# One outer product of a fast-weight recurrence, moved from GpSimd to VectorE

## The chip, the cores and the metric

The kernel runs on one core of a Trainium2 chip. Its time is the device time of one execution in microseconds (us). A core has five engines, each with an instruction queue of its own that it works off strictly in order: TensorE (PE, its weight loads PEld) for matrix products into PSUM, VectorE (DVE), ScalarE (ACT), GpSimd (POOL), and SyncE (SP), which issues the DMA transfers here. Engines wait for one another through semaphores. In the profile, L534 is line 534 of the kernel.

## The reference

Two blocks are applied to x of shape 16 x 512 x 256 (batch, time, channels). The second block (attention in a window of 64 and a gated mixing of channels) and the low-rank feed-forward network of the first are not touched. The part that matters is the attention of the first block, a recurrence over chunks of 16 tokens with 16 heads of 16 channels. Each head carries two small matrices of 4 inner rows, `W_in` and `W_out`:

```python
def step(carry, xs):
    W_in, W_out = carry
    q_t, k_t, v_t, lr_t = xs
    ...
    W_out = W_out + jnp.einsum('bnhD,bnhd->bDhd', k_h, v_t)
    lr_in = lr_t[:, :1, :, 0:1]
    lr_out = lr_t[:, :1, :, 1:2]
    for _ in range(2):
        g_out = -attn(W_in, k_t, v_t)
        g_in = -attn(W_out, v_t, k_t)
        W_in = W_in - lr_in * g_in
        W_out = W_out - lr_out * g_out
    return ((W_in, W_out), o_t)
```

`attn(W_out, v_t, k_t)` scores the 4 rows of `W_out` against the 16 tokens `v_t`, takes the softmax over the tokens, and sums the tokens `k_t` with these weights. It is used twice in a step, with two successive `W_out`; both sums are added to `W_in`. Nothing of a step can start before the `W_in` and `W_out` that it needs are there.

## The kernel before

A unit of work is one half of the batch (8 sequences) and 64 time steps; there are 16 units, which alternate between the halves. A unit goes through five streams: `prepare` (norm, projections, convolution), `chain` (the recurrence, 4 chunks of 16 tokens, `recur`), `mlp`, `attend` and `mix`. `timetable` gives each stream its times, so that in the text of the program the chains of two units, one of each half, run side by side, while earlier and later units go through the other streams. The scheduler of the language then orders each engine's instructions by its own estimate of when they can run, so the order on an engine is not that of the text.

In the recurrence the 128 partitions are the 8 sequences by 16 heads of one half. A product of 4 rows, 16 channels and 16 tokens is 1024 elements for each partition. A sum over tokens is made in two instructions: `outer` (L530 to L535) multiplies weights and tokens, both spread by broadcasting, into a buffer, on GpSimd; `total` (L634 to L637) sums that buffer over its last axis on VectorE. Scores (L523 to L528) are a product and a reduction, both on VectorE. The matrices `w_in` and `w_out` (tile `fw`) lie in PSUM; the tokens, the weights and the product buffers lie in SBUF. The product buffers are a ring of five for both halves (`big`, L520).

A step does this in order:

- L602 to L613: scores of k and q with `w_in`, the first softmax (weights `e_k`), the softmax over inner rows (`hid`).
- L615 and L626: two outer products on GpSimd, `pd_o` and `pd_kv`.
- L628 to L632: `pd_kv` is summed up along the tokens with a scan on VectorE.
- L641 to L644: `w_out` after the first inner step; scores of v with both versions of `w_out`, and exponentials `e_v` for both (2 x 4 rows).
- L646: `over_tokens` turns `e_v` into weights; its last instruction is L549.
- L647: the two outer products `pd_i`, one for each inner step, with the tokens `dt_k`, both on GpSimd. In the text the first stands before the second.
- L649: the sum `di` of the first product (L636) is added to `w_in`.
- L651 and L652: scores of k with this `w_in`, and the exponentials of the second softmax.
- L653: the sum of the second product is added to `w_in`. This is the `w_in` of the next step.
- L655 and L657: the last outer product `pd_o` on GpSimd; its sum is added to `w_out` early in the next step.
- L661 to L663: the outputs of the chunk, three products and sums on GpSimd.

GpSimd also adds residuals (`x` L389), squares (`ka` L1055), copies the rows that the convolution carries over (`xp` L453, `tails` L456), splits maxima (L215 and L217) and takes the root for the norms (`rs` L350 and L351). VectorE also does the convolution (L460), the maxima of the attention's scores (L889), the mixing (`mix` L1033), and norms (L347, L348, L353).

Of the kernel before, what the change touches and what calls it, by code (L numbers as in the profile page):

```python
# [17 lines left out]
P = 128  # L18
B, T, C = 16, 512, 256
H, D, R = 16, 16, 4  # L20
CH = 16
# [74 lines left out]
def adaln_blocks(ctx: ExitStack, tc: tile.TileContext, a: dict, out: bass.AP):  # L96
    nc = tc.nc
    mul, add, sub = ALU.mult, ALU.add, ALU.subtract
# [295 lines left out]
    def place(u):  # L394

        return u % NH, u // NH
# [120 lines left out]
    def small(half, name, n):  # L517
        return rec.tile([P, n], F32, tag=f"s{n}_{half}", name=name, bufs={XW: 5, 2 * XW: 3}.get(n, 4))

    def big(half, name):  # L520
        return rec.tile([P, R * D * CH], F32, tag="prod", name=name, bufs=5)

    def scores(half, engine, tok, w, dst, tag):  # L523

        pr = big(half, f"sc_{tag}").rearrange("p (r t d) -> p r t d", r=R, t=CH)
        every = [P, R, CH, D]
        engine.tensor_tensor(pr, tok.unsqueeze(1).to_broadcast(every), w.unsqueeze(2).to_broadcast(every), mul)  # L527
        nc.vector.tensor_reduce(dst, pr, AX.X, add)  # L528

    def outer(half, engine, hid, tok, tag):  # L530

        pr = big(half, f"pd_{tag}").rearrange("p (r d t) -> p r d t", r=R, d=D)
        every = [P, R, D, CH]
        engine.tensor_tensor(pr, hid.unsqueeze(2).to_broadcast(every), tok.unsqueeze(1).to_broadcast(every), mul)  # L534
        return pr  # L535

    def exp_tokens(half, s, n, mx, tag):

        nc.vector.tensor_reduce(mx, s, AX.X, ALU.max)
        e = small(half, f"e_{tag}", n * CH).rearrange("p (r t) -> p r t", t=CH)  # L540
        nc.vector.tensor_tensor(e, s, mx.unsqueeze(2).to_broadcast([P, n, CH]), sub)
        nc.scalar.activation(e, e, AF.Exp, scale=1.0 / math.sqrt(D))
        return e

    def over_tokens(half, e, n, rate, sm):

        nc.vector.tensor_reduce(sm, e, AX.X, add)
        nc.vector.reciprocal(sm, sm)
        nc.vector.scalar_tensor_tensor(e, e, rate, sm.unsqueeze(2).to_broadcast([P, n, CH]), mul, mul)  # L549
        return e  # L550
# [36 lines left out]
    def recur(u, pc, c, s):  # L587

        half = place(u)[0]
        f = fws[half]  # L590
        tag = f"{u}_{pc}_{c}"
        cs = slice(c * CH, (c + 1) * CH)
        k_dt, v_dt, q_dt, lr = s["k"][:, :, cs], s["v"][:, :, cs], s["q"][:, :, cs], s["lr"]
        lr_in, lr_out = lr[:, 0, c * CH : c * CH + 1], lr[:, 1, c * CH : c * CH + 1]
        tok = rec.tile([P, 3, CH, D], F32, tag=f"tok_{half}", name=f"tok{tag}", bufs=1)
        for n, x in enumerate((k_dt, q_dt, v_dt)):
            nc.scalar.copy(tok[:, n], x.rearrange("p d t -> p t d"))  # L597
        k, q, v = (tok[:, n] for n in range(3))
        w_in, w_out, w_outs = f["w_in"], f["w_out"], f["w_outs"]

        sc = small(half, f"scs{tag}", 2 * XW).rearrange("p (r t) -> p r t", r=R)
        scores(half, nc.vector, k, w_in, sc[:, :, :CH], f"k{tag}")  # L602
        scores(half, nc.vector, q, w_in, sc[:, :, CH:], f"q{tag}")
        late[half]()
        p_out = exp_tokens(half, sc[:, :, :CH], R, f["mx_k"], f"k{tag}")


        mx = f["hid"]
        nc.vector.tensor_reduce(mx, sc.rearrange("p r t -> p t r"), AX.X, ALU.max)
        hid = small(half, f"hid{tag}", R * 2 * CH).rearrange("p (r t) -> p r t", r=R)  # L610
        every = [P, R, 2 * CH]
        nc.vector.tensor_tensor(hid, sc, mx.unsqueeze(1).to_broadcast(every), sub)
        nc.scalar.activation(hid, hid, AF.Exp)  # L613
        yield
        d_out = outer(half, nc.gpsimd, over_tokens(half, p_out, R, lr_out, f["sm_k"]), v_dt, f"o1{tag}")  # L615

        sm = f["hid"][:, :CH]
        kh, qh = hid[:, :, :CH], hid[:, :, CH:]
        nc.vector.tensor_reduce(sm, kh.rearrange("p r t -> p t r"), AX.X, add)
        nc.vector.tensor_reduce(s["sum"][:, cs], qh.rearrange("p r t -> p t r"), AX.X, add)  # L620
        nc.vector.reciprocal(sm, sm)
        nc.vector.tensor_tensor(sm, sm, lr[:, 1, cs], mul)
        nc.vector.tensor_tensor(kh, kh, sm.unsqueeze(1).to_broadcast([P, R, CH]), mul)  # L623


        kv = outer(half, nc.gpsimd, kh, v_dt, f"kv{tag}")  # L626
        yield
        nc.vector.tensor_tensor(kv[:, :, :, 0], kv[:, :, :, 0], w_out, add)  # L628
        upto = kv
        flat = kv.rearrange("p r d t -> p (r d t)")  # L630
        nc.vector.tensor_tensor_scan(flat, within, flat, 0.0, mul, add)  # L631
        nc.vector.tensor_copy(w_outs[:, :R], upto[:, :, :, CH - 1])  # L632

        def total(pr, name):  # L634
            t = small(half, f"{name}{tag}", XW).rearrange("p (r d) -> p r d", r=R)
            nc.vector.tensor_reduce(t, pr, AX.X, add)  # L636
            return t  # L637


        sv = small(half, f"sv{tag}", 2 * XW).rearrange("p (r t) -> p r t", t=CH)  # L640
        nc.vector.tensor_tensor(w_outs[:, R:], total(d_out, "do1"), w_outs[:, :R], add)  # L641
        for n in range(2):
            scores(half, nc.vector, v, w_outs[:, n * R : (n + 1) * R], sv[:, n * R : (n + 1) * R], f"v{n}{tag}")
        p_in = exp_tokens(half, sv, 2 * R, f["mx_v"], f"v{tag}")  # L644
        yield
        p_in = over_tokens(half, p_in, 2 * R, lr_in, f["sm_v"])  # L646
        d_in = [outer(half, nc.gpsimd, p_in[:, n * R : (n + 1) * R], k_dt, f"i{n}{tag}") for n in range(2)]  # L647
        yield
        nc.vector.tensor_tensor(w_in, total(d_in[0], "di0"), w_in, add)  # L649
        sk = small(half, f"sk{tag}", XW).rearrange("p (r t) -> p r t", t=CH)  # L650
        scores(half, nc.vector, k, w_in, sk, f"k2{tag}")  # L651
        p_out = exp_tokens(half, sk, R, f["mx_k"], f"k2{tag}")  # L652
        nc.vector.tensor_tensor(w_in, total(d_in[1], "di1"), w_in, add)  # L653
        yield
        d_out = outer(half, nc.gpsimd, over_tokens(half, p_out, R, lr_out, f["sm_k"]), v_dt, f"o2{tag}")  # L655
        yield
        late[half] = lambda: nc.vector.tensor_tensor(w_out, total(d_out, "do2"), w_outs[:, R:], add)  # L657


        po = upto  # L660
        nc.gpsimd.tensor_tensor(po, qh.unsqueeze(2).to_broadcast([P, R, D, CH]), upto, mul)  # L661
        nc.gpsimd.tensor_tensor(po[:, :2], po[:, :2], po[:, 2:], add)
        nc.gpsimd.tensor_tensor(q_dt, po[:, 0], po[:, 1], add)  # L663
# [435 lines left out]
    def chain(u):  # L1099

        for m in range(NPC):
            piece = load_piece(u, m)
            for c in range(CPP):
                yield from recur(u, m, c, piece)
                if c == CPP - 1:
                    finish_piece(u, m, piece)
                yield
# [87 lines left out]
```

## Time and profile before

| | us |
|---|---|
| time, median of 3 runs | 3226.88 |
| lowest and highest of them | 3222.9 and 3235.52 |
| the profiled execution's own time | 3231.29 |
| its span, first to last instruction | 3229.5 |
| mean granted TensorE clock in it | 0.822 |

Three more groups of the recurrence, as the page has them:

```profile
L534 POOL TENSOR_TENSOR pd_o<-e_k,dt_v 128x1024 f32<-128x1024 f32 x128 | 301.0, 2358 | 171.4 <-DVE e_k L549 171.3
...
L661 POOL TENSOR_TENSOR pd_kv<-hid,pd_kv 128x1024 f32<-128x1024 f32 x64 | 150.3, 2349 | 165.6 <-DVE fw L632 141.6
...
L631 DVE TENSOR_TENSOR_SCAN pd_kv<-within,pd_kv 128x1024 f32<-128x1024 bf16 x64 | 174.4, 2725 | 0.9
```

A line gives the source line, the engine, the operation, output and inputs by name, their shapes, the count; then the busy time of the group in us and the mean of one in ns; then the idle time of the engine just before these instructions, and what ended it. The first line says that 128 outer products took 301.0 us on GpSimd, and that GpSimd had stood idle 171.4 us in front of them, nearly all of it for the weights `e_k` from VectorE. In a timeline a line gives start and duration in us first, and in brackets the idle time before it with its releaser. In a line by source or tile, the three numbers after the count are the least, the median and the greatest duration in ns.

### The profile page before, as it was taken

The page shows a single profiled execution, that of the slowest core. Times are in us where ns is not written, and L with a number is a line of the kernel's source. Part 1 is how long each engine was busy: PE and PEld are TensorE (multiplying, and loading weights), DVE is VectorE, ACT ScalarE, POOL GpSimd, SP SyncE. Part 2 cuts the span into 40 slices and gives each one's busy share as a digit, 9 for nine tenths or more (in the row PEclk, how much of TensorE's full clock was granted, in tenths as well). Part 3 has the DMA queues.
Part 4 walks back from the last instruction along what each step waited for, and adds up shares of the span by engine and source line. Part 5 has one row for each costly group of instructions (what it writes and reads, how often), then busy time and mean ns, then how long its engine had stood idle before and what let it go on. Part 6 is the DMA issues. An engine that isn't in the chain of part 4 may idle for free.

```text
span 3229.5 us, 47324 instructions
## 1 busy us (share of the span) xinstructions
PE 2385.4 (74%) x17232; PEld 1452.9 (45%) x17232; DVE 2395.3 (74%) x4513; ACT 1783.6 (55%) x3748; POOL 1673.0 (52%) x1575
## 2 busy tenths in 40 slices
PE   3540156868787776887788887889787888788996
PEld 2210123444444454554445554555445555555664
DVE  1688787878787787778888888888888878774221
ACT  1761354556665745565564666566664655445543
POOL 0245556556556655555556564555555655654112
PEclk7775676878797887888888798979888887879998
DMA  5420112132314132131313223230402212122010
GB/s 151 94 58 13 47 37 67 31 73 55 80 36 94 32 83 54 51 83 33 88 27 72 69 59 75 51 83 27 100 21 72 62 51 56 45 52 60 17 28 27
DMA packets 439307, 186.46 MB, mean 58 GB/s; under 512 B 323937, under 2 KB 413090, under 8 KB 439074
## 3 DMA queue, kind: packets, MB, share of 16 engines
q1 hardware_dynamic: 439074, 183.44, 23.2%
q8 instruction: 135, 2.21, 0.3%
q14 instruction: 98, 0.80, 0.1%
HBM read 116.66 MB, written 66.72 MB: 57 GB/s over the span
## 4 chain that ended last, share of the span: by engine, by line
DVE 33%; PE 22%; POOL 20%; ACT 12%; issue 8%; DMA 4%; SPq 1%; POOLq 0%; DVEq 0%; ACTq 0%
POOL pd_o L534 5%; POOL pd_i L534 4%; DVE pd_kv L631 4%; DVE sc_v L527 3%; POOL pd_kv L534 3%; DVE sv L528 3%; DVE do L636 2%; PE st L873 2%; DVE di L636 2%; DVE sc_k L527 2%; DVE pp L460 2%; PE pproj L1005 2%; DMA oT<-o 2%; DVE scs L528 2%; DVE mx L889 1%
## 5 line engine op out<-in xcount | busy, mean ns | idle before, releaser
L534 POOL TENSOR_TENSOR pd_o<-e_k,dt_v 128x1024 f32<-128x1024 f32 x128 | 301.0, 2358 | 171.4 <-DVE e_k L549 171.3
L534 POOL TENSOR_TENSOR pd_i<-e_v,dt_k 128x1024 f32<-128x1024 f32 x128 | 298.4, 2369 | 43.4 <-DVE e_v L549 43.4
L708 PE MATMUL pwo<-w_WoT,oT 128*128 128x256 f32 x256 | 106.6, 576 | 223.0 <-POOL oT L701 201.8
L873 PE MATMUL st<-qs,keys 32*128 32x128 f32 x2048 | 191.3, 336 | 71.7 <-DVE yT L983 29.0
L661 POOL TENSOR_TENSOR pd_kv<-hid,pd_kv 128x1024 f32<-128x1024 f32 x64 | 150.3, 2349 | 165.6 <-DVE fw L632 141.6
L873 PE MATMUL sc<-keys,qs 32*128 32x128 f32 x2048 | 183.1, 326 | 71.7 <-DVE mx L889 41.7
L636 DVE TENSOR_REDUCE do<-pd_o 128x64 f32<-128x1024 f32 x126 | 152.3, 1213 | 102.5 <-POOL pd_o L534 102.5
L636 DVE TENSOR_REDUCE di<-pd_i 128x64 f32<-128x1024 f32 x128 | 155.1, 1214 | 88.3 <-POOL pd_i L534 88.3
L873 PEld LDWEIGHTS st<-qs,keys 32*128 32x128 f32 x2048 | 160.5, 226 | 132.2 <-DVE mx L889 32.4
L873 PEld LDWEIGHTS sc<-keys,qs 32*128 32x128 f32 x2048 | 148.0, 216 | 141.9 <-DVE mx L889 58.8
L889 DVE TENSOR_REDUCE mx<-sc 128x4 f32<-128x512 f32 x256 | 168.2, 679 | 26.2 <-PE sc L870 26.2
L708 PEld LDWEIGHTS pwo<-w_WoT,oT 128*128 128x128 f32 x256 | 68.4, 287 | 250.7 <-POOL oT L701 218.3
L534 POOL TENSOR_TENSOR pd_kv<-hid,dt_v 128x1024 f32<-128x1024 f32 x64 | 151.4, 2366 | 54.7 <-DVE hid L623 50.0
L926 ACT ACTIVATE pT<-st 128x512 f32<-128x512 f32 x256 | 135.3, 605 | 73.7 <-PE st L870 73.4
L631 DVE TENSOR_TENSOR_SCAN pd_kv<-within,pd_kv 128x1024 f32<-128x1024 bf16 x64 | 174.4, 2725 | 0.9
L527 DVE TENSOR_TENSOR sc_k<-tok,fw 128x1024 f32<-128x1024 f32 x128 | 155.4, 1214 | 14.8 <-ACT tok L597 13.5
L527 DVE TENSOR_TENSOR sc_v<-tok,fw 128x1024 f32<-128x1024 f32 x128 | 150.3, 1215 | 1.6
L224 ACT ACT_TABLE_LOAD x111 | 142.4, 1283 | 14.3 <-PE ph L736 7.6
L528 DVE TENSOR_REDUCE sv<-sc_v 128x64 f32<-128x1024 f32 x128 | 149.6, 1209 | 0.0
L736 PE MATMUL ph<-PT,w_v 64*128 64x512 f32 x256 | 111.1, 669 | 38.0 <-ACT z L224 27.8
L1005 PE MATMUL pproj<-w_proj,yT 128*128 128x256 f32 x512 | 122.9, 386 | 11.2 <-DVE yT L983 9.3
L197 PE MATMUL pmx<-w_w_attnT,blocks 128*128 128x384 f32 x256 | 118.5, 593 | 13.4 <-ACT hp L367 9.4
(251 smaller groups left out, 6827.7 us busy)
## 6 DMA issues: line engine op xcount, KB each, us to landing
values<-values SPq DMA_DIRECT2D x56, 256.0 KB
gate_a<-gates SPq DMA_DIRECT2D x64, 128.0 KB
xa<-in_x_dram SPq DMA_DIRECT2D x32, 256.0 KB
x<-in_x_dram SPq DMA_DIRECT2D x32, 256.0 KB
gate_c<-gates SPq DMA_DIRECT2D x64, 128.0 KB
gate_d<-gates SPq DMA_DIRECT2D x64, 128.0 KB
q<-y SPq DMA_DIRECT2D x64, 128.0 KB
dt_q<-q SPq DMA_DIRECT2D x32, 256.0 KB
```

The costliest lines, as they stand in the source:

```text
L224: ins = nc.scalar.activation(*args[0], **args[1])
L527: engine.tensor_tensor(pr, tok.unsqueeze(1).to_broadcast(every), w.unsqueeze(2).to_broadcast(every), mul)
L528: nc.vector.tensor_reduce(dst, pr, AX.X, add)
L534: engine.tensor_tensor(pr, hid.unsqueeze(2).to_broadcast(every), tok.unsqueeze(1).to_broadcast(every), mul)
L631: nc.vector.tensor_tensor_scan(flat, within, flat, 0.0, mul, add)
L636: nc.vector.tensor_reduce(t, pr, AX.X, add)
L661: nc.gpsimd.tensor_tensor(po, qh.unsqueeze(2).to_broadcast([P, R, D, CH]), upto, mul)
L708: nc.tensor.matmul(po[:, n * C : (n + 1) * C], lhsT=pair(oT, k, 2 * b2 + n), rhs=w_o[:, k, :], start=k == 0, stop=k == 1,)
L873: nc.tensor.matmul(dst, lhsT=lhsT, rhs=rhs, start=start, stop=False, skip_group_check=True)
L889: nc.vector.tensor_reduce(mx[:, j], sc[j].rearrange("p (s k) -> p s k", s=NS), AX.X, ALU.max)
L926: nc.scalar.activation(pT[j], st[j], AF.Exp)
L1005: nc.tensor.matmul(po[:, n * C : (n + 1) * C], lhsT=yT[:, k2, par].rearrange("p e t -> p (e t)"), rhs=w_proj[:, k2, par, :], start=k2 == 0 ...
```

## The change

`outer` takes a list of engines instead of one, and shares the 4 inner rows out among them in equal parts. The first `pd_i` gets the list with VectorE alone, the second the list with GpSimd alone; all other outer products get GpSimd alone. With a list of one, `n` is 4 and the product is one instruction of 1024 elements as before. In the changed kernel the multiplication of `outer` is at L537, the last instruction of `over_tokens` at L554, `total` at L641, and the additions to `w_in` at L657 and L661.

```diff
-    def outer(half, engine, hid, tok, tag):
+    def outer(half, engines, hid, tok, tag):
 
         pr = big(half, f"pd_{tag}").rearrange("p (r d t) -> p r d t", r=R, d=D)
-        every = [P, R, D, CH]
-        engine.tensor_tensor(pr, hid.unsqueeze(2).to_broadcast(every), tok.unsqueeze(1).to_broadcast(every), mul)
+        n = R // len(engines)
+        every = [P, n, D, CH]
+        for k, engine in enumerate(engines):
+            part = slice(k * n, (k + 1) * n)
+            engine.tensor_tensor(
+                pr[:, part], hid[:, part].unsqueeze(2).to_broadcast(every), tok.unsqueeze(1).to_broadcast(every), mul
+            )
         return pr
...
-        d_in = [outer(half, nc.gpsimd, p_in[:, n * R : (n + 1) * R], k_dt, f"i{n}{tag}") for n in range(2)]
+        d_in = [
+            outer(half, engines, p_in[:, n * R : (n + 1) * R], k_dt, f"i{n}{tag}")
+            for n, engines in enumerate(([nc.vector], [nc.gpsimd]))
+        ]
```

The other three calls (`o1`, `kv`, `o2`) change `nc.gpsimd` to `[nc.gpsimd]` and nothing else.

More of the change, by code (lines that the diff above doesn't have):

```diff
@@ L614, in recur @@
         yield
-        d_out = outer(half, nc.gpsimd, over_tokens(half, p_out, R, lr_out, f["sm_k"]), v_dt, f"o1{tag}")
+        d_out = outer(half, [nc.gpsimd], over_tokens(half, p_out, R, lr_out, f["sm_k"]), v_dt, f"o1{tag}")
         sm = f["hid"][:, :CH]
@@ L623, in recur @@
         nc.vector.tensor_tensor(kh, kh, sm.unsqueeze(1).to_broadcast([P, R, CH]), mul)
-        kv = outer(half, nc.gpsimd, kh, v_dt, f"kv{tag}")
+        kv = outer(half, [nc.gpsimd], kh, v_dt, f"kv{tag}")
         yield
@@ L654, in recur @@
         yield
-        d_out = outer(half, nc.gpsimd, over_tokens(half, p_out, R, lr_out, f["sm_k"]), v_dt, f"o2{tag}")
+        d_out = outer(half, [nc.gpsimd], over_tokens(half, p_out, R, lr_out, f["sm_k"]), v_dt, f"o2{tag}")
         yield
```

## The prediction

> **What bounds the kernel now.** I read the page first: busy shares, the slices, the chain that ended last, the costliest groups.
>
> ```profile
> PE 2385.4 (74%) x17232; PEld 1452.9 (45%) x17232; DVE 2395.3 (74%) x4513; ACT 1783.6 (55%) x3748; POOL 1673.0 (52%) x1575
> ...
> DVE  1688787878787787778888888888888878774221
> ...
> DVE 33%; PE 22%; POOL 20%; ACT 12%; issue 8%; DMA 4%; SPq 1%; POOLq 0%; DVEq 0%; ACTq 0%
> POOL pd_o L534 5%; POOL pd_i L534 4%; DVE pd_kv L631 4%; DVE sc_v L527 3%; POOL pd_kv L534 3%; DVE sv L528 3%; DVE do L636 2%; PE st L873 2%; DVE di L636 2%; DVE sc_k L527 2%; DVE pp L460 2%; PE pproj L1005 2%; DMA oT<-o 2%; DVE scs L528 2%; DVE mx L889 1%
> ...
> L534 POOL TENSOR_TENSOR pd_i<-e_v,dt_k 128x1024 f32<-128x1024 f32 x128 | 298.4, 2369 | 43.4 <-DVE e_v L549 43.4
> ...
> L636 DVE TENSOR_REDUCE di<-pd_i 128x64 f32<-128x1024 f32 x128 | 155.1, 1214 | 88.3 <-POOL pd_i L534 88.3
> ...
> L527 DVE TENSOR_TENSOR sc_k<-tok,fw 128x1024 f32<-128x1024 f32 x128 | 155.4, 1214 | 14.8 <-ACT tok L597 13.5
> ```
>
> VectorE is 70 to 80% busy from slice 3 until the recurrence ends, and it stands first in the chain. GpSimd is half idle, but what VectorE waits for is often a GpSimd product: 88.3 us of idle time stand before the reductions `di`. So the span is VectorE's queue, its work plus its waits. Then I read the timeline where the change acts. The two halves of the batch run in step: 30 pairs of steps, and 4 single ones at the ends. This is a pair with no other work between:
>
> ```profile
> 1105.58 0.35 DVE L549 SCALAR_TENSOR_TENSOR e_v<-e_v,lr,fw 128x128 f32<-128x128 f32 x1
> 1108.38 1.22 DVE L636 TENSOR_REDUCE di<-pd_i 128x64 f32<-128x1024 f32 x1 [2.46 <-POOL pd_i L534]
> ...
> 1112.99 1.22 DVE L636 TENSOR_REDUCE di<-pd_i 128x64 f32<-128x1024 f32 x1 [1.04 <-POOL pd_i L534]
> ...
> 1106.00 9.25 POOL L534 TENSOR_TENSOR pd_i<-e_v,dt_k 128x1024 f32<-128x1024 f32 x4 [3.04 <-DVE e_v L549]
> ```
>
> GpSimd starts 0.07 us after the weights `e_v` are done and needs 9.25 us for four products; VectorE idles 2.46 and 1.04 us. A VectorE instruction that depends on the one before it follows after about 0.04 us.
>
> The third reading is of VectorE instructions whose two tensor inputs both lie in SBUF, as those of the moved product will (`e_v` and `dt_k`; the scores read their weights from PSUM). By line (min/median/max ns), and one case:
>
> ```profile
> L631 DVE TENSOR_TENSOR_SCAN pd_kv<-within,pd_kv x64: 2254/2291/4407, 142.2 to 2935.7; 128x1024 f32<-128x1024 bf16 x64
> ...
> L353 DVE SCALAR_TENSOR_TENSOR off_c<-mv_c,rs_c x16: 152/164/2322, 454.7 to 3074.2; 128x4 f32<-128x4 f32 x16
> ...
> 624.81 2.32 POOL L534 TENSOR_TENSOR pd_kv<-hid,dt_v 128x1024 f32<-128x1024 f32 x1
> ...
> 624.87 2.28 DVE L353 SCALAR_TENSOR_TENSOR off_c<-mv_c,rs_c 128x4 f32<-128x4 f32 x1 [1.04 <-POOL rs_c L351]
> ```
>
> Four elements need 0.16 us alone and 2.28 us when GpSimd's product started 0.06 us earlier: it ends with that product. The scan grows from 2.29 to at most 4.41 us, by about one product.
>
> [...] the row of `sc_k` has 1214, which I use.
>
> **The change part by part.** Despite its words nothing is divided: each list holds one engine, so n is R. The first product, whole, goes to VectorE; the second stays.
>
> *Removed:* 64 of 128 `pd_i` from GpSimd, 64 x 2.35 = 150 us of an engine that has slack. *Added:* 64 products on VectorE at 1.214 + 0.04 = 1.25 us, 80 us, all on the path. *Idle removed:* `di` of a first product no longer waits; `di` of a second waits for a product that starts where the first did, some 2.3 us sooner. I take all 88.3 us. Without a port the balance would be 80 - 88 = -8.
>
> *The port.* GpSimd's second product waits for the same `e_v` as VectorE's first. In the changed program's instruction order, what stands between `e_v` and its product on VectorE decides. Nothing: VectorE is there after 0.04 us, GpSimd after 0.07; VectorE wins and GpSimd's product, needed 3 us later, is late without harm. Something: GpSimd is 2.3 us deep and VectorE stands blocked, with all its queue behind it: the other half's weights, the scores, convolutions and maxima that ACT and PE wait for. Bounds for one product: 0 and 2.3 us. By the order, with idle read pair by pair from the timeline:
> - Nothing between, 7 pairs and 3 single steps, 17 products: idle -31.0, work +21.3, blocked 0 (the other half's product arrives at 3.5 us, when GpSimd's delayed one ends): -9.7.
> - Second product behind a `mix` multiply, 7 pairs: the `mix`, itself with two SBUF inputs, is held 0.45 us, then GpSimd takes the port and the product waits 2.2; against that the `mix` is held about 0.9 already (1.68 for 0.74 us at 2032). 7 x 1.75 = +12.3, idle -20.9, work +17.5: +8.9.
> - Convolution step (0.75) ahead of the first, a reduction (1.21) ahead of the second, 7 pairs: blocked 2.35 - 0.75 and 2.35 - 1.2, 2.7 with rounding: +18.9, idle -16.4, work +17.5: +20.0.
> - A short step ahead of each, 5 pairs; one of them:
>
> ```profile
> 1186.40 0.34 DVE L549 SCALAR_TENSOR_TENSOR e_v<-e_v,lr,fw 128x128 f32<-128x128 f32 x1
> 1186.78 0.69 DVE L387 TENSOR_TENSOR up_c<-pproj,gate_c 128x512 f32<-128x512 f32 x1
> ...
> 1192.75 0.43 DVE L347 BATCH_NORM_STATS2 st_d<-x 128x6 f32<-128x256 f32 x1 [2.05 <-POOL x L389]
> ...
> 1186.83 4.66 POOL L534 TENSOR_TENSOR pd_i<-e_v,dt_k 128x1024 f32<-128x1024 f32 x2
> ```
>
>   Blocked 1.6 and 1.85, some 3 on average: +15, idle -5.6, work +12.5: +21.9.
> - The other 4 pairs and a step, 9 products: one in each waits about 1.9: +9.5, idle -14.6, work +11.3: +6.2.
>
> Sum: work 80 + port 56 - idle 88 = +47 us.
>
> *Moved.* GpSimd work queued behind four products now stands behind two. In three such pairs VectorE waits 2.05 us for `x` (above) and about 1.3 for `rs_d`, once 4.6 for `rs_d`: -15. ACT and PE run ahead while VectorE is late, so waits on them shrink (in 300 to 2950 us `pp` has 34, `up_a` 21, `yT` 21); I take -12, an estimate, bounds 0 and -30. A product's buffer may have to wait for GpSimd's last read of `kv`; that ended at 1102.96, 3 us before `e_v`: nothing. No DMA is added; SP keeps its transfers. Sum: +47 - 15 - 12 = +20 us.
>
> The profiled execution took 3231.3 us (span 3229.5 and 1.8 around it), the median is 3226.9. 3231.3 + 20 = 3251; the same on the median: 3247, +0.6%.
>
> **The rivals.**
> 1. *VectorE gets the port (faster).* If VectorE is served ahead of queued GpSimd products, or GpSimd comes late because its queue is behind, blocking vanishes: 80 - 88 - 15 = -23 us, 3204. It decides at a mean block below (88 + 15 - 80)/64 = 0.36 us a product; I have 56/64 = 0.88. For it: the 17 clean products. Against: wherever GpSimd began 0.06 us earlier, VectorE waited it out.
> 2. *GpSimd gets it also in the clean cases.* The lead is 0.03 us; if the port is taken later than the instruction starts, 17 products wait 2.2 us more: +37, so +57, 3284. For it: the small lead. Against: scans that started while GpSimd was idle ran at 2.29.
> 3. *The new order pays or costs elsewhere.* About a fifth of VectorE's instructions stand elsewhere relative to one another. The scheduler put fillers by its own costs; a gain of 20 us elsewhere gives no change, 3227. For it: `do` waits of 102.5 us, which placement decides. Against: nothing in the order aims at them.
>
> **How the numbers follow.** A comparison of this kernel can tell about 0.5%, 16 us. Mine (+5 to +35) 0.43; rival 1 0.24; rival 2 0.16; rival 3 0.17. Slower by over 0.5%: 0.34 of mine and rival 2, 0.50; within: the rest of mine and rival 3, 0.26; faster 0.24. The likeliest is 3247, its own range 3232 to 3262; to hold 8 in 10 it must reach rivals 1 and 2: 3198 to 3292.
>
> **What would show it.** Right: 64 `pd_i` on VectorE at a mean near 2.1 us, minimum 1.2, maximum about 3.5; `di` idle under 15 us; VectorE busy 2395 + 80 + 56, about 2530; GpSimd busy about 1525, more where its products record waiting. A mean of 1.3 us is rival 1, of 2.7 rival 2. If VectorE's busy time rises as said and the time does not, the absorption was undersized; if `di` keeps 40 us or more, the idle I removed was not there to take.

## The result, and the profile after

The change makes the kernel 1.3% slower: 3270.76 us (median of 4 runs, 3267.89 to 3273.23) against 3228.6 us for the kernel before in the same comparison (4 runs, 3222.9 to 3235.52). The ratio is 1.0129, with a 95% interval of 1.0107 to 1.0152: +42 us. The profiled execution of the changed kernel took 3267.89 us, its span is 3266.1 us, 36.6 us longer than that of before.

The page of the changed kernel: busy time, VectorE's slices, the chain that ended last, and the groups of the moved product.

```profile
PE 2403.7 (74%) x17232; PEld 1471.8 (45%) x17232; DVE 2507.9 (77%) x4577; ACT 1762.7 (54%) x3736; POOL 1564.1 (48%) x1511
...
DVE  1689888888888897778888888888889888875221
...
DVE 39%; PE 21%; POOL 16%; ACT 11%; issue 10%; DMA 3%; SPq 1%; POOLq 0%; DVEq 0%; ACTq 0%
...
L537 POOL TENSOR_TENSOR pd_i<-e_v,dt_k 128x1024 f32<-128x1024 f32 x64 | 176.7, 2765 | 74.9 <-DVE e_v L554 74.4
...
L641 DVE TENSOR_REDUCE di<-pd_i 128x64 f32<-128x1024 f32 x128 | 154.7, 1208 | 0.1
...
L537 DVE TENSOR_TENSOR pd_i<-e_v,dt_k 128x1024 f32<-128x1024 f32 x64 | 149.6, 2338 | 1.4
```

The chain moved from GpSimd (20% to 16%) to VectorE (33% to 39%). The idle time before `di` fell from 88.3 us to 0.1. In its place stand 149.6 us of products. 64 such products cost 78.1 us at the 1.22 us of one that nothing holds; the other 71.5 us are time in which VectorE was held, 1.12 us for each product.

The balance of VectorE (its busy and its idle time make up the span): busy +112.6 (2395.3 to 2507.9), idle -76.0 (834.2 to 758.2), together +36.6. By item: products +149.6, idle before `di` -88.2, all the rest -24.8 (busy -37.0, idle +12.2). Here, time in which the records of two VectorE instructions overlap is counted once.

How the hold looks is seen in the line of the tile and in two stretches of the timeline. By tile (least, median, greatest duration in ns):

```profile
L537 DVE TENSOR_TENSOR pd_i<-e_v,dt_k x64: 1210/2469/3405, 151.8 to 2993.2; 128x1024 f32<-128x1024 f32 x64
L537 POOL TENSOR_TENSOR pd_i<-e_v,dt_k x64: 2323/2380/3397, 151.8 to 2993.3; 128x1024 f32<-128x1024 f32 x64
```

Timeline of the changed kernel, a pair with a convolution step between `e_v` and the first product, and a pair with nothing between:

```profile
1569.23 0.35 DVE L554 SCALAR_TENSOR_TENSOR e_v<-e_v,lr,fw 128x128 f32<-128x128 f32 x1
...
1569.49 0.75 DVE L460 SCALAR_TENSOR_TENSOR pp<-xp,w_ck,pp 128x512 f32<-128x512 f32 x1
...
1569.66 2.38 POOL L537 TENSOR_TENSOR pd_i<-e_v,dt_k 128x1024 f32<-128x1024 f32 x1 [0.68 <-DVE e_v L554]
...
1570.15 2.97 DVE L537 TENSOR_TENSOR pd_i<-e_v,dt_k 128x1024 f32<-128x1024 f32 x1
```

```profile
754.42 0.35 DVE L554 SCALAR_TENSOR_TENSOR e_v<-e_v,lr,fw 128x128 f32<-128x128 f32 x1
...
754.80 1.22 DVE L537 TENSOR_TENSOR pd_i<-e_v,dt_k 128x1024 f32<-128x1024 f32 x1
754.84 3.37 POOL L537 TENSOR_TENSOR pd_i<-e_v,dt_k 128x1024 f32<-128x1024 f32 x1 [3.05 <-DVE e_v L554]
...
758.93 0.35 DVE L554 SCALAR_TENSOR_TENSOR e_v<-e_v,lr,fw 128x128 f32<-128x128 f32 x1
759.35 2.35 POOL L537 TENSOR_TENSOR pd_i<-e_v,dt_k 128x1024 f32<-128x1024 f32 x1 [1.14 <-DVE e_v L554]
...
759.38 3.40 DVE L537 TENSOR_TENSOR pd_i<-e_v,dt_k 128x1024 f32<-128x1024 f32 x1
```

In the first stretch GpSimd begins at 1569.66, and VectorE's product, which begins at 1570.15, ends 1.08 us after GpSimd's. That is the case that was forecast. The second was forecast to cost nothing: in the first half's step VectorE came first and GpSimd's product was stretched to 3.37 us without harm, but in the other half's step GpSimd began 0.03 us before VectorE, and VectorE's product took 3.40 us in place of 1.22.

### The profile page after: what moved, and what is told of

Same layout as the page of the kernel before. It is cut to its first block, busy times and chain, and to the rows that moved or that the text cites. A ratio compares the mean times of both kernels' runs of the same rounds, so it can differ in the third digit from the quotient of the medians.

```text
span 3266.1 us, 47350 instructions
## 1 busy us (share of the span) xinstructions
PE 2403.7 (74%) x17232; PEld 1471.8 (45%) x17232; DVE 2507.9 (77%) x4577; ACT 1762.7 (54%) x3736; POOL 1564.1 (48%) x1511
## 4 chain that ended last, share of the span: by engine, by line
DVE 39%; PE 21%; POOL 16%; ACT 11%; issue 10%; DMA 3%; SPq 1%; POOLq 0%; DVEq 0%; ACTq 0%
POOL pd_o L537 5%; DVE pd_i L537 4%; DVE pd_kv L636 4%; DVE sc_v L527 3%; POOL pd_kv L537 3%; DVE sv L528 3%; PE pproj L1013 2%; DVE sc_k L527 2%; DVE di L641 2%; DVE scs L528 2%; DVE do L641 2%; PE ph L744 2%; DVE pp L460 2%; DVE mx L897 2%; PE pp L441 1%
## 5 line engine op out<-in xcount | busy, mean ns | idle before, releaser
L537 POOL TENSOR_TENSOR pd_o<-e_k,dt_v 128x1024 f32<-128x1024 f32 x128 | 299.3, 2344 | 256.7 <-DVE e_k L554 256.7
L716 PE MATMUL pwo<-w_WoT,oT 128*128 128x256 f32 x256 | 113.9, 608 | 244.3 <-POOL oT L709 210.8
L881 PE MATMUL st<-qs,keys 32*128 32x128 f32 x2048 | 198.2, 332 | 69.3 <-DVE mx L897 37.0
L641 DVE TENSOR_REDUCE do<-pd_o 128x64 f32<-128x1024 f32 x126 | 153.0, 1215 | 124.0 <-POOL pd_o L537 124.0
L881 PEld LDWEIGHTS st<-qs,keys 32*128 32x128 f32 x2048 | 169.6, 223 | 128.9 <-DVE mx L897 61.3
L537 POOL TENSOR_TENSOR pd_i<-e_v,dt_k 128x1024 f32<-128x1024 f32 x64 | 176.7, 2765 | 74.9 <-DVE e_v L554 74.4
L537 POOL TENSOR_TENSOR pd_kv<-hid,dt_v 128x1024 f32<-128x1024 f32 x64 | 154.1, 2408 | 60.5 <-DVE hid L628 56.2
L641 DVE TENSOR_REDUCE di<-pd_i 128x64 f32<-128x1024 f32 x128 | 154.7, 1208 | 0.1
L537 DVE TENSOR_TENSOR pd_i<-e_v,dt_k 128x1024 f32<-128x1024 f32 x64 | 149.6, 2338 | 1.4
L528 DVE TENSOR_REDUCE sv<-sc_v 128x64 f32<-128x1024 f32 x128 | 149.6, 1209 | 0.0
L1013 PE MATMUL pproj<-w_proj,yT 128*128 128x256 f32 x512 | 128.6, 395 | 10.2 <-DVE yT L991 9.5
```

Source lines behind the costliest of these rows:

```text
L537: engine.tensor_tensor(pr[:, part], hid[:, part].unsqueeze(2).to_broadcast(every), tok.unsqueeze(1).to_broadcast(every), mul)
L716: nc.tensor.matmul(po[:, n * C : (n + 1) * C], lhsT=pair(oT, k, 2 * b2 + n), rhs=w_o[:, k, :], start=k == 0, stop=k == 1,)
L881: nc.tensor.matmul(dst, lhsT=lhsT, rhs=rhs, start=start, stop=False, skip_group_check=True)
L1013: nc.tensor.matmul(po[:, n * C : (n + 1) * C], lhsT=yT[:, k2, par].rearrange("p e t -> p (e t)"), rhs=w_proj[:, k2, par, :], start=k2 == 0 ...
```

## The experiments

Two theories. *Port*: the time lost is VectorE's hold behind GpSimd's second product. (Port is the author's name for what the two engines would share; the traces show the hold and not what lies behind it.) *Order*: the change redraws the order of instructions on every engine, and that, not the hold, makes the difference. (In the trace of before, all 4513 instructions of VectorE, all 1575 of GpSimd and the 3516 of ScalarE that are not table loads start in the order of the program.) Runs of before stood beside all kernels; their medians were 3229.5 to 3233.7.

### The hold by itself: the second product waits

```diff
-        d_in = [outer(... for n, engines in enumerate(([nc.vector], [nc.gpsimd])))]
+        d_in = [outer(half, [nc.vector], p_in[:, :R], k_dt, f"i0{tag}")]
+        first = made[half]
+        d_in.append(outer(half, [nc.gpsimd], p_in[:, R:], k_dt, f"i1{tag}"))
+        tc.add_manual_dep(made[half].ins, first.ins.name, ...)
```

`made[half]` is the product that `outer` issued last. GpSimd's second product now starts only when VectorE's first has ended; no work is added.

> The change with one wait added: GpSimd's second product of a half waits for VectorE's first product of the same half, so that GpSimd does not hold the port when VectorE comes. Theory of the port: VectorE's product falls from 2.34 to 1.3 to 1.5 us, 55 to 65 us are saved against the change, about 3210 us (3195 to 3225), under the kernel before; the reductions of second products still do not wait. Rival (the product takes 2.34 us by itself, or the new order costs): duration 2.3 us as in the change, time 3271 or a little more, since GpSimd starts later.

Measured: 3192.24 us (3189.44 to 3204.94), ratio to before 0.9886 (0.9856 to 0.9917). That is 79 us below the change, slightly past the expected stretch, and faster than both kernels. Page and tile view of this kernel:

```profile
PE 2378.5 (74%) x17232; PEld 1459.3 (46%) x17232; DVE 2447.0 (76%) x4577; ACT 1762.9 (55%) x3736; POOL 1530.5 (48%) x1511
```

```profile
L539 DVE TENSOR_TENSOR pd_i<-e_v,dt_k x64: 1210/1224/2714, 152.6 to 2929.1; 128x1024 f32<-128x1024 f32 x64
L539 POOL TENSOR_TENSOR pd_i<-e_v,dt_k x64: 2321/2348/2402, 153.9 to 2931.1; 128x1024 f32<-128x1024 f32 x64
its engine sat idle before it (us, times) until:
  DVE pd_i L539: 125.6, 43
```

The median product fell from 2469 to 1224 ns, and the sum of the 64 from 149.6 to 87.2 us. GpSimd idles 125.6 us for VectorE, and the span is shorter all the same. All 4577 VectorE and all 3736 ScalarE instructions stand in the same order as in the change (on GpSimd 28 of 1511 stand elsewhere, on TensorE 8 of 17232 matmuls), so a new order is hardly the reason: one added wait took 63 us off the span (79 off the median), and the hold that it took away is 62. In this order the span fell by what VectorE was held for.

### Other ways to share the work

Only the lists of engines change: both products on VectorE; the first split by rows between the two engines (`[nc.gpsimd, nc.vector]`) and the second on GpSimd; the first on GpSimd and the second on VectorE.

```diff
-            for n, engines in enumerate(([nc.vector], [nc.gpsimd]))
+            for n, engines in enumerate(([nc.vector], [nc.vector]))
```

> Both products of a step on VectorE, so 128 instead of 64 there and none on GpSimd at that moment. Theory of the port (VectorE is held only while GpSimd reads): the product falls from 2.34 us on average to at most 1.4, so 128 x 1.3 = 166 us of VectorE work against 88 us of idle time removed and about 25 us given back elsewhere: about +55 us against the kernel before, 3283 us (3265 to 3300). Rival (such a product simply takes 2.34 us on VectorE, whatever GpSimd does): 300 - 88 - 25 = +187 us, 3415. Rival (the scheduler's new order is what costs, not the product): no reason for the duration to fall, and a time near that of the change, 3271, or anywhere.

Measured: 3268.88 us (3260.68 to 3278.38), ratio 1.0117 (1.0084 to 1.015), within the expected stretch. The 128 products have a median of 1220 ns: with no GpSimd product of the same weights to meet they are hardly held (15.5 us in all). The kernel is as slow as the change: a second set of 64 products, 78 us, stands where the change has 71.5 us of hold.

> The first product as the words of the change have it: two inner rows on GpSimd and two on VectorE, the second product on GpSimd. Theory of the port: VectorE's half is 512 elements, 0.69 us alone, and is held whenever GpSimd's half or whole product is in front, so a mean of 1.3 to 2.0 us; 64 x 1.7 = 109 us against at most 88 us of idle time: 3225 to 3265 us. Rival (without a port the halves run side by side): mean 0.7 us, 45 us of work against some 60 us of idle time removed, 3205 to 3220 us.

Measured: 3233.08 us (3227.55 to 3245.19), ratio 1.0005 (0.9991 to 1.0019): no difference. VectorE's half product takes 1034 ns in the mean where the shortest takes 681, so 22.6 us of hold; the idle time before `di` falls only to 53.3. Both sides of the exchange are smaller, and the forecast mean of 1.3 to 2.0 us was too high.

> First product on GpSimd, second on VectorE. Theory of the port: VectorE is held as in the change (mean 1.9 to 2.5 us) and now the reduction of the first product also waits for GpSimd, whose product is held when VectorE comes first, so di idles 30 to 80 us: 3275 to 3320 us, no better than the change. Rival (the cost is VectorE's added work alone): the work fills the time in which VectorE waited for the first product, so the time falls under 3229.

Measured: 3297.22 us (3296.67 to 3299.89), ratio 1.0205 (1.0181 to 1.023), in the expected stretch. The product on VectorE is the second one here, and in 57 of 64 cases GpSimd was already at work when it began:

```profile
L537 DVE TENSOR_TENSOR pd_i<-e_v,dt_k x64: 1210/3177/3390, 151.6 to 3023.9; 128x1024 f32<-128x1024 f32 x64
```

A mean of 2744 ns, more than expected, 98 us of hold, and still 20.8 us of idle time before `di`, less than expected. The split, the change and this kernel stand in the order of their hold: 22.6, 71.5, 98 us at 3233, 3271, 3297. Each has also work and an order of its own, so this agrees with *port* and does not prove it.

### The hold taken away by another memory

The trace of before has VectorE instructions of both kinds that began while a GpSimd instruction ran on for 0.3 us or more. The `mix` multiplies, whose two tensor inputs lie in SBUF, took 1.71 us there in the median (1.40 to 2.65, 9 cases) against 0.744 with no GpSimd instruction beside them (38 cases). The scores `sc_k`, which read their weights from PSUM, took 1.214 us (1.200 to 1.222, 62 cases) against 1.220 (46 cases). If the weights of the moved product lie in PSUM, it too has one tensor input in SBUF. They get one of the three PSUM banks of pool `ps`, so before and change were run with two banks as well.

```diff
-    ps = ctx.enter_context(tc.tile_pool(name="ps", bufs=3, space=PSUM))
+    ps = ctx.enter_context(tc.tile_pool(name="ps", bufs=2, space=PSUM))
```

> The kernel before with two instead of three rotating PSUM banks for its general tiles: the yardstick for the next two runs, which need one bank. Slower than before by some unknown amount, on TensorE's side: 3235 to 3330 us. The theories don't differ here.

Measured: 3319.19 us (3318.38 to 3324.39), ratio 1.0267 (1.0249 to 1.0284), in the expected stretch.

> The change with two instead of three rotating PSUM banks: the second yardstick. By both theories 25 to 55 us above the run of the kernel before with two banks, VectorE's product at 2.1 to 2.5 us on average.

Measured: 3282.62 us (3279.86 to 3290.49), ratio 1.0154 (1.013 to 1.0179). A miss: with two banks the change is not slower than before but 37 us faster.

```diff
-            outer(half, engines, p_in[:, n * R : (n + 1) * R], k_dt, f"i{n}{tag}")
-            for n, engines in enumerate(([nc.vector], [nc.gpsimd]))
+            outer(half, [nc.vector], first, k_dt, f"i0{tag}"),
+            outer(half, [nc.gpsimd], p_in[:, R:], k_dt, f"i1{tag}"),
```

`first` lies in the bank that was freed; the last instruction of `over_tokens` is split in two, one for each destination.

> The change with two banks, and the weights of the first product written to the freed PSUM bank (their last instruction is divided into one for the first product's rows and one for the second's), so VectorE's product has one SBUF input and GpSimd's second product starts at once as in the change. Theory of the port: VectorE's product takes 1.21 to 1.3 us every time, 70 us less work; 64 more short instructions at 0.27 us less the shorter of the old one, +12 us; so 45 to 80 us below the change with two banks. Rival (it is GpSimd's being busy or the product itself that makes it long, wherever its inputs lie): mean 2.3 us and a time some 10 us above the change with two banks.

Measured: 3306.02 us (3295.04 to 3310.84), ratio 1.0218 (1.0192 to 1.0244).

The products of the change with two banks, then those of this kernel:

```profile
L537 DVE TENSOR_TENSOR pd_i<-e_v,dt_k x64: 1195/1422/3410, 154.9 to 2970.9; 128x1024 f32<-128x1024 f32 x64
```

```profile
L538 DVE TENSOR_TENSOR pd_i<-ew,dt_k x64: 1193/1219/1227, 154.6 to 3000.8; 128x1024 f32<-128x1024 f32 x64
L538 POOL TENSOR_TENSOR pd_i<-e_v,dt_k x64: 2322/2337/2374, 154.8 to 3000.0; 128x1024 f32<-128x1024 f32 x64
```

None of the 64 products is held (1227 ns at most), though GpSimd's run beside them: the first of each start at 154.6 and 154.8 us, and the last on VectorE, at 3000.8, falls into GpSimd's of 3000.0. GpSimd's own are not stretched either (2374 ns at most). So with the weights in PSUM the hold of up to 2.2 us is gone. But the time is 23 us above the change with two banks, not 45 to 80 below. VectorE's busy time fell by 13.6 us (2493.7 to 2480.1, with 64 more instructions), its idle time rose by 41 (788 to 829). The products are 46.9 us shorter, but 13.7 us go into the divided instruction and 12.1 into scans (`pd_kv`) that take longer here. How much of the idle time comes from the extra instruction on the path and how much from the new order stays open. So this run shows that the hold went when one input left SBUF, not what the hold costs.

### The order by itself

Two kernels of before change nothing but the order, and after the two misses the same was done to the change. The times of one stream in the text were shifted by 0.03 of a unit: the mixing in one pair, the feed-forward network in the other.

```diff
-        yield mix, [(8, u + 4.1, u + 4.7)]
+        yield mix, [(8, u + 4.13, u + 4.73)]
```

```diff
-        yield mlp, [(10, u + 2, u + 2.65)]
+        yield mlp, [(10, u + 2.03, u + 2.68)]
```

> The kernel before with the due times of the stream mix moved by 0.03 of a unit and nothing else, so the scheduler puts fillers elsewhere. Theory of the port: no statement, but the time of such a reordering should lie within 15 us of before, 3215 to 3245. Rival (the order is what moves this kernel by 40 us): a change of 25 us or more in either direction.

Measured: 3303.21 us (3297.4 to 3305.84), ratio 1.0211 (1.0192 to 1.0231). A miss: 70 us more with the same products on the same engines (ScalarE has 4 table loads fewer, 3744 instructions in place of 3748).

> The kernel before, with the feed-forward network of each unit placed 0.03 of a unit later in the text; no work is added, removed or moved between engines. Theory 'order': an arbitrary reordering alone moves this kernel by some tens of us, as the later mixing did (+70): 25 us or more away from 3230, of either sign. Theory 'one bad spot': the later mixing was an exception, and this one lies within 15 us of 3230.

Measured: 3308.82 us (3307.69 to 3313.37), ratio 1.0242 (1.0222 to 1.0263): the first shift was no exception. The granted TensorE clock was lower here too, 0.799 to 0.809 in the four runs against 0.82 to 0.827 in the runs of before beside them. TensorE's busy time did not grow (2383.6 us against 2385.4), but whether the clock has a part in the 75 us was not tested. With two banks the clock was 0.818 to 0.824, and 86 us were lost all the same.

> The change, with the mixing of each unit 0.03 of a unit later in the text, as was done to the kernel before (3303). Theory 'port': the change costs the same in every order, so this is 20 to 60 us above 3303, 3323 to 3363, with VectorE's 64 products at a mean of 2.1 to 2.6 us. Theory 'order': the VectorE products are held for as long, but the shift acts on the change in its own way: within 30 us of 3271, and so below the same shift of the kernel before.

Measured: 3326.32 us (3325.66 to 3329.99), 23 us above before with that shift; products at a mean of 2107 ns.

> The change, with the feed-forward network of each unit 0.03 of a unit later in the text. Theory 'port': 20 to 60 us above the same shift of the kernel before, with VectorE's products at a mean of 2.1 to 2.6 us. Theory 'order': the mean is the same, but the difference to the same shift of the kernel before lies outside 20 to 60, of either sign.

Measured: 3287.94 us (3285.32 to 3298.5), 21 us below before with that shift; products at a mean of 2012 ns, just under the expected 2.1 to 2.6 us. In the first pair the *port* theory's figures hold, in the second the *order* theory's.

### The wait in the other orders

> The change with the later mixing, in which GpSimd's second product waits for VectorE's first. Both theories: the hold goes from VectorE's products (mean 1.3 to 1.5 us against 2.1 to 2.6) in this order too. Theory 'port': the gain is that of the first order, 60 to 95 us below the change with the later mixing. Theory 'luck': the 78 us were in part a chance of that order, and here the gain is below 40 us.

Measured: 3313.3 us (3302.86 to 3320.0), only 13 below the change with that shift: the figures of the theory 'luck'.

> The change with two PSUM banks and the wait of GpSimd's second product; to be set against the change with two banks, 3282.6, where VectorE's products were held 46 us. Theory 'full price': every us of hold that the wait removes comes off the time, as in the first order: hold down by 30 to 40, time 3240 to 3255. Theory 'cover': the order decides how much of it other waits take up, as with the later mixing: hold down by the same, time anywhere from 3240 to 3283, with VectorE's idle time growing by what is not gained.

Measured: 3253.57 us (3245.74 to 3256.22), 29 below the change with two banks. This lies in the stretch of either theory.

> The change with the later feed-forward network and the wait of GpSimd's second product; to be set against the change with that shift, 3287.9, where VectorE's products were held 49 us. Theory 'full price': hold down by 35 to 45, time 3243 to 3258. Theory 'cover': hold down by the same, time anywhere from 3243 to 3290, with VectorE's idle time growing by what is not gained.

Measured: 3259.92 us (3254.07 to 3265.01), 28 below the change with that shift: just outside the stretch of a full price, inside that of cover.

All four orders side by side (with two banks a PSUM bank is missing besides; median us; the rows join runs of several comparisons, whose medians of before differed by up to 5 us), then what the wait did in each: the sum of VectorE's 64 products, its idle time, the span, and the median.

| order | before | change | change with the wait | before to change | before to wait |
|---|---|---|---|---|---|
| as written | 3228.6 | 3270.8 | 3192.2 | +42 | -36 |
| mixing later | 3303.2 | 3326.3 | 3313.3 | +23 | +10 |
| feed-forward later | 3308.8 | 3287.9 | 3259.9 | -21 | -49 |
| two banks | 3319.2 | 3282.6 | 3253.6 | -37 | -66 |
| mean | 3290.0 | 3291.9 | 3254.8 | +2 | -35 |

| change to wait | products | VectorE idle | span | median |
|---|---|---|---|---|
| as written | -62.4 | -2.1 | -63.0 | -79 |
| mixing later | -42.6 | +26.9 | -7.7 | -13 |
| feed-forward later | -33.0 | +10.8 | -20.8 | -28 |
| two banks | -34.4 | +2.9 | -30.1 | -29 |

In all four orders the wait takes most of the hold away; what it is worth differs, and the idle time shows where the rest goes. With the mixing later, three waits of VectorE for other engines grew. First the change with that shift, then the same with the wait (the numbers after the colon are the sum in us, the times, and the longest):

```profile
DVE mx L897 <- PE sc L878: 27.6, 6, 11.0
...
DVE qs L625 <- ACT hid L618: 19.0, 14, 2.2
...
DVE fw L552 <- ACT e_k L547: 15.1, 15, 3.4
```

```profile
DVE mx L904 <- PE sc L885: 36.9, 12, 9.5
...
DVE fw L554 <- ACT e_k L549: 27.3, 17, 5.5
DVE qs L627 <- ACT hid L620: 25.9, 13, 4.4
```

9.3, 12.2 and 6.9 us, 28 together, are about the whole growth of the idle time (26.9). There VectorE comes early to work that TensorE and ScalarE have not finished; in the order as written it does not (-2.1). So the hold has no single price: at the profiled spans it came off at 101, 18, 63 and 88% (span over products). A full price meets two of the four orders and fails in the other two, so that theory falls; that of cover stands.

The same view shows where the sign of the change comes from, though not why. VectorE's busy time rises by much the same in all four orders (112.6, 105.4, 119.1, 117.4 us), and the idle time before `di` that it can remove is much the same (88.3, 96.5, 91.8, 94.7). What differs is all idle time together: it falls by 76.0, 85.3, 141.9 and 152.3. Before, as written, has the least of it, 834.2 us, where the three neighbours have 920.7, 924.3 and 940.4. So the change was measured against the best of the four orders. Part of its +42 may be what other orders lose against that one as well; no run tells these parts from one another.

## Why the prediction missed

The forecast was 3247, +20, and +42 came. The hold came as forecast, VectorE's product behind GpSimd's, and the time lies in the wide range (3198 to 3292), but the range of the forecast's own case (3232 to 3262) did not. That the sign held is in part luck: in two of four orders it is the other one. By its own steps:

- *Work on VectorE, 80*: right. An unheld product takes 1.22 us and follows `e_v` after 0.034.
- *Idle before `di`, -88.3*: right, 88.2.
- **The port, +56**: this is the step that failed. It measured 71.5. That an instruction which begins behind GpSimd's waits it out is in the trace of before: all 17 of `off_a` to `off_d` that began 0.06 us after a GpSimd product took 2.28 to 2.34 us and ended 0.016 to 0.023 us after it. In the changed kernel 45 products began behind a GpSimd instruction and were held; the other 19 took 1.21 to 1.23 us. By the classes of the forecast, taking a product above 1.22 us as held:

| class | forecast | measured |
|---|---|---|
| nothing between | 0 | 7.1 |
| second behind `mix` | 12.3 | 15.0 |
| convolution, reduction | 18.9 | 20.2 |
| short step ahead of each | 15 | 19.0 |
| the other products | 9.5 | 10.2 |

  The largest error is "Nothing between ... blocked 0". It rests on "VectorE is there after 0.04 us, GpSimd after 0.07", read from instructions that wait for VectorE alone. In the changed program VectorE's second product of every other pair waits for two semaphores, VectorE's and, for its buffer, GpSimd's. Such a product started 0.104 us after `e_v` and not 0.034, GpSimd's after 0.08, and in 3 of the 7 clean pairs (and in one more pair) VectorE lost 2.2 us. (In three other clean pairs it started as late, but GpSimd was still at work on its product for the other half.) The forecast had priced that wait at nothing: "A product's buffer may have to wait for GpSimd's last read ... nothing". The read had indeed ended; the wait still cost 0.07 us of start, and that turned over who came first.

  The traces show why. With two waits, the one for VectorE's own last result stands in an instruction of its own ahead of the product (`EVENT_SEMAPHORE`), which ends about 0.04 us before the product starts. In the trace of before, all 748 VectorE instructions that stood idle for VectorE's own result alone started 0.033 to 0.036 us after it. Of those with the extra instruction none started before 0.102 us, and 53 after 0.102 to 0.104. In the changed kernel these are 680 after 0.033 to 0.036 us and 47 after 0.103 to 0.105. The number of waits did not decide it: ten convolution steps (`y`) of these two traces wait for three semaphores, but carry the wait for VectorE themselves, and started after 0.035 to 0.036 us. So the price of the start could be read before the change was run. A kernel in which the products are free of that second wait was not run.

  In the short-step pairs each product lost about 1.9 us (19.0 over 10); the forecast had 1.6 and 1.85 and rounded the pair down to 3.
- *Relief of GpSimd's queue and absorption, -27*: the size came out, -24.8, but by luck, for the composition did not. The waits for `rs_d` and `x` fell (about 12 and 9), those on `pp` and `up_a` too (17 and 14), but `ss_k`, `do`, `ss_q`, `up_c` and `ov` waited 91 us more in all, so the idle time outside `di` rose by 12. What fell instead is the busy time of other VectorE instructions, by 37: their records are 21.5 us shorter in sum (`off_c` 10.8 and `mix` 10.5 us the most, both held by GpSimd in the trace of before: `off_c` 2.28 us for 0.16, `mix` up to 2.65 for 0.74), and the other 15.5 us are records that overlap more.
- On the span the port makes 15 of the 16.6 us between forecast (+20) and measurement (+36.6). The other 5 up to +42 lie between a profiled execution and its median: that of before was above its median, that of the change below.

The rivals. *VectorE gets the port* was put at 3204 and was to decide below 0.36 us of hold for each product: the change has 1.12, the kernel with the wait 0.14, and that ran at 3192, so its price was about right for that kernel, and its condition is not met in the change. *GpSimd gets it in the clean cases* came true for 3 of 17 products. *The order* was given 20 us of effect. That was far too little: three small changes to before, two of them shifts of 0.03 of a unit, moved it by 70 to 86 us against before as written, and the change without the hold stands between 10 us above and 66 below before, by order. In the order as written what was predicted besides the port, 80 - 88 - 27 = -35, meets the -36 of the kernel with the wait; a mean of -35 over four orders agrees, but with single values so far apart this may be chance. How much of the -36 is exchange of work for idle time, and how much the order, stays open. Shown is that in this order the hold takes the change from faster to slower; over four orders the change is worth +2 us in the mean, with single values from -37 to +42.

## What to carry to other kernels

Before an elementwise product with two SBUF inputs goes from GpSimd to VectorE, see what GpSimd will run at that moment: here it started a product from the same release, VectorE paid up to 2.2 us for it, and one wait that held back the product needed later was worth more than the move (3271 to 3192). Read the start for such a race from instructions that wait in the same way, extra wait instructions included. And where a scheduler orders the queues, compare a change with its neighbours too: shift something harmless in both kernels and see whether the sign survives; here it did not, while the wait gained in all four orders, by 13 to 79 us.

## What was not expected of the hardware

- A lead of about 0.025 us decided a loss of 2.2 us (3.40 us for a product, 1.22 where VectorE led by 0.045). The starts after `e_v` were 0.034 us for a product that waits for VectorE alone, 0.104 where the wait for VectorE stands in an instruction of its own, and 0.08 for GpSimd.
- A held product did not cost the whole sum. 3.40 us for a start 0.03 behind GpSimd's 2.35 us and 1.22 of its own: VectorE ended 1.08 us after the recorded end of GpSimd's. All 45 held products of the changed kernel ended 1.08 to 1.09 us after it, 0.14 less than the 1.22 of an unheld one.
- The hold was mutual: where VectorE came first, by 0.045 to 0.048 us, GpSimd's product grew from 2.35 us to between 3.36 and 3.40 (17 cases).
